# RWKV in three interleaved pieces, roots by logarithm and exponential, norms on ScalarE: a change to a two-layer Perceiver kernel

## The chip, the cores and the metric

The kernel runs on one core of a Trainium2 chip. The core has five engines with queues of their own: TensorE (PE in the profile, with its weight loads as PEld), VectorE (DVE), ScalarE (ACT), GpSimd (POOL) and SyncE (SP), which here only issues transfers. Each engine takes its instructions in the order in which the program lists them. The metric is the device time of one execution in microseconds (us).

## The reference, cut to what matters

The input is x of shape 64 x 32 x 256 and a context of 64 x 257 x 256. Six residual steps follow one another, each on a layer norm of x:

```python
x = x + L0_xattn(_layernorm(x), ctx, ctx, mask)      # stage 0: attention on the context
x = x + L0_attn(_layernorm(x), ...)                  # stage 1: RWKV
x = x + L0_ffn(_layernorm(x), Wg, We, be)            # stage 2: 8 experts, the best 2
x = x + L1_xattn(_layernorm(x), ctx, ...)            # stage 3: quantized attention
x = x + L1_attn(_layernorm(x), ...)                  # stage 4: state-space scan
x = x + L1_ffn(_layernorm(x), ...)                   # stage 5: 8 experts, all of them
return x
```

Stage 1, which the change cuts in three, has a time mix and a channel mix:

```python
h = layernorm(x, ln1_g, ln1_b); hh = time_shift(h)
xk, xv, xr = (h * m + hh * (1 - m) for m in (tm_k, tm_v, tm_r))
k, v, sr = xk @ Wk.T, xv @ Wv.T, sigmoid(xr @ Wr.T)
x = x + (sr * wkv(time_decay, time_first, k, v)) @ Wo.T       # a recurrence over 32 steps
h = layernorm(x, ln2_g, ln2_b); hh = time_shift(h)
xk, xr = (h * m + hh * (1 - m) for m in (cm_k, cm_r))
x = x + sigmoid(xr @ Wcr.T) * (square(relu(xk @ Wck.T)) @ Wcv.T)
```

## The kernel before

The 2048 rows (64 x 32) are cut into four blocks of 512 rows, each held in SBUF as four tiles of 128 rows x 256. x stays in SBUF from the first stage to the last. Every stage is a function that handles one block; `layers` (L1188) lists which stage of which block is written when, and a scheduler of the framework then puts each engine's instructions in an order of its own, with this list as priority. So stages of different blocks run mixed: stage 0 of one block beside stage 1 of the one before, and later stage 3 of one block beside the scan of stage 4 of another and the experts of stage 5 of a third.

Stage 0 (`_stage0`, L136) loads the context for four rows of the batch at a time (16 groups), and for each group computes the quantization scales of the context (L209), stores them to DRAM by a transfer on ACT's queue (L224), loads them back spread over the partitions, multiplies on POOL (L230), and attends (L236), with ACT doing exponentials and emptying PE's banks.

Stage 1 (`_stage1`, L340) is one function `block` per block (L470). It norms x, transposes it to channels (`norm_to`, L418), mixes with the shifted rows (L391), projects to k, v and r, runs the recurrence for two halves of the channels (`recur`, L432, mostly DVE, with a scratch pool of nine tiles), then projects back (`wo`, L490), norms again, and does the channel mix: `cr` (L503), then eight times `ck` (L511), Relu on ACT (L513), a square on POOL (L514) and `cv` (L523), all of the same block, in one go.

A norm is one DVE instruction (`_norm`, L114, and L429), x minus the mean times a reciprocal root; one set of four in stage 1 stands on POOL (L485). The mean and the variance come from L101 and L102. The reciprocal root (`_rsqrt`, L76) is a shift and a subtraction on the bits of the number, done on DVE (L84 to L87), and three Newton steps of four small instructions each on POOL (L89 to L92). A root for two sets of constants at once goes through it as one tile of eight columns.

Stage 4 has `ahead` (L968: norm, projection, convolution, softplus with an ACT logarithm at L1017 and an exponential at L1019), `gates` (L1026: four times Silu, straight from PE's bank, L1030) and `recur` (L1032): for 16 states POOL makes the input g (L1048), ACT the decay (L1052), DVE scans (L1053) and multiplies (L1054), and POOL sums (L1055); at the end it norms x and adds the output projection (L1062 to L1073). Stage 5 (L1081) has Gelu on ACT (L1164) between two rows of matmuls (L1160, L1168). ACT's functions come in tables; an instruction that loads one stands ahead of a function that the present table lacks.

Of the kernel before, what the change touches and what calls it, by code (L numbers as in the profile page):

```python
# [15 lines left out]
P = 128  # L16
# [39 lines left out]
def _consts(k):  # L56
    nc, c = k.nc, k.const
    k.ident = c.tile([P, P], F32, name="ident", tag="ident")
    make_identity(nc, k.ident)
    k.identb = c.tile([P, P], BF16, name="identb", tag="identb")  # L60
    nc.vector.tensor_copy(k.identb, k.ident)
    k.ones = c.tile([P, P], F32, name="ones", tag="ones")
    nc.gpsimd.memset(k.ones, 1.0)

    k.bmask = c.tile([P, 4], F32, name="bmask", tag="bmask")
    nc.vector.tensor_reduce(k.bmask, k.ident.rearrange("p (j n) -> p j n", n=32), AX.X, ALU.add)
    k.chan = c.tile([P, NCHAN], F32, name="chan", tag="chan")
    nc.scalar.dma_start(k.chan, k.i["chan"])
# [6 lines left out]

def _rsqrt(k, out, parts, tag, pool=None):  # L76


    nc, pool, f = k.nc, pool or k.small, out.shape[-1]
    n = out.shape[0]  # L80
    v, r, t = (pool.tile([P, f], F32, name=f"rs_{q}", tag=f"rs_{q}{tag}")[:n] for q in "vrt")
    at = 0
    for in_, scale, eps in parts:
        nc.vector.tensor_scalar(v[:, at : at + in_.shape[-1]], in_, scale, eps, ALU.mult, ALU.add)  # L84
        at += in_.shape[-1]
    nc.vector.tensor_scalar(r.bitcast(I32), v.bitcast(I32), 1, None, ALU.logical_shift_right)
    nc.vector.tensor_scalar(r.bitcast(I32), r.bitcast(I32), -1.0, 1597463007.0, ALU.mult, ALU.add)  # L87
    for step in range(3):
        nc.gpsimd.tensor_tensor(t, r, r, ALU.mult)  # L89
        nc.gpsimd.tensor_tensor(t, t, v, ALU.mult)  # L90
        nc.gpsimd.tensor_scalar(t, t, -0.5, 1.5, ALU.mult, ALU.add)
        nc.gpsimd.tensor_tensor(out if step == 2 else r, r, t, ALU.mult)  # L92

# [12 lines left out]
def _stats(k, tiles, tag, pool=None):  # L106

    mv = _moments(k, tiles, tag, pool)
    rstd = (pool or k.small).tile([P, 4], F32, name="rstd", tag=f"rstd{tag}")
    _rsqrt(k, rstd, [(mv[:, :, 1], 1.0, LN_EPS)], tag, pool)  # L110
    return mv, rstd


def _norm(k, out, x, mv, rstd, j):  # L114
    k.nc.vector.tensor_scalar(out, x, mv[:, j, 0:1], rstd[:, j : j + 1], ALU.subtract, ALU.mult)

# [19 lines left out]
def _stage0(k, pool):  # L136
# [163 lines left out]
    def steps():  # L300

        def of(dq, a, s, tag):
            _rsqrt(k, dq, [(s, 1.0 / D, RMS_EPS)], tag, blk)
            nc.vector.tensor_tensor(dq, dq, a, ALU.mult)
            nc.vector.tensor_scalar(dq, dq, 1e-5, 1.0 / 127.0, ALU.max, ALU.mult)
# [34 lines left out]
def _stage1(k, pool):  # L340
# [4 lines left out]
    nc, i = k.nc, k.i  # L345
    w, u, wk, sm1 = pool("w1", 1), pool("u1", 9), pool("wk1", 1), pool("small1", 2)
    pa, pb = pool("psa1", 2, space=bass.MemoryType.PSUM), pool("psb1", 2, space=bass.MemoryType.PSUM)
# [19 lines left out]
    for c in range(2):  # L367
# [4 lines left out]
        e2b.append(padded(f"e2b{c}", 0.0))  # L372
        e2bv.append(padded(f"e2bv{c}", 0.0))
    hT = padded("hT", 0.0, (2, 16, T + 1))

# [12 lines left out]
    def rows(name):  # L388
        return wk.tile([P, 4, D], F32, name=name, tag="rows", bufs=3)

    def shift_mix(names):  # L391


        def mix(name):
            return wk.tile([P, 2, 16, T], F32, name=name, tag="mix", bufs=3)

# [20 lines left out]

    def norm_to(xs, mean, scale, g, b):  # L418

# [8 lines left out]
        for j in range(4):  # L428
            nc.vector.tensor_scalar(hn[:, j, :], xs[:, j, :], mean[:, j, :], scale[:, j : j + 1], ALU.subtract, ALU.mult)  # L429
        _to_channels(k, [hn[:, j, :] for j in range(4)], evac, lambda shape, name: ps(name))  # L430
# [38 lines left out]

    def block(b):  # L470
        x = k.x[b]
# [4 lines left out]
        r8 = sm1.tile([P, 8], F32, name="r8", tag="r8")  # L476
        _rsqrt(k, r8, [(mv[:, :, 1], 1.0, LN_EPS), (mv[:, :, 1], 1.0 + LN_EPS, LN_EPS * LN_EPS)], "1", sm1)
        norm_to(x, mv[:, :, 0:1], r8[:, 4:8], "L0_attn_ln1_g", "L0_attn_ln1_b")
        xk, xv, xr = shift_mix(["L0_attn_tm_k", "L0_attn_tm_v", "L0_attn_tm_r"])
        rw = wk.tile([P, 2, BT], F32, name="rw", tag="rw", bufs=1)  # L480
        for c in range(2):
            recur(c, xk, xv, xr, rw)
        xn = rows("xn")
        for j in range(4):
            nc.gpsimd.tensor_scalar(xn[:, j, :], xs[j], mv[:, j, 0:1], r8[:, j : j + 1], ALU.subtract, ALU.mult)  # L485
        for j in range(0, 4, 2):
# [7 lines left out]

        mv2, rstd2 = _stats(k, [xn[:, j, :] for j in range(4)], "1b", sm1)
        norm_to(xn, mv2[:, :, 0:1], rstd2, "L0_attn_ln2_g", "L0_attn_ln2_b")
        xk, xr = shift_mix(["L0_attn_cm_k", "L0_attn_cm_r"])
        sg = rows("sg")
        for j in range(0, 4, 2):
            p = pa.tile([P, 2, D], F32, name="cr", tag="a")  # L500
            for f in range(2):
                for c in range(2):
                    nc.tensor.matmul(p[:, f, :], xr[:, c, (j + f) * P : (j + f + 1) * P], wT["cr"][:, c, :], start=c == 0, stop=c == 1)  # L503
            nc.scalar.activation(sg[:, j : j + 2, :], p, AF.Sigmoid)

        cvs = [pb.tile([P, 2, D], F32, name="cv", tag="b") for _ in range(2)]
# [23 lines left out]

    return block

# [120 lines left out]
def _stage3(k, w, tmp):  # L653
# [33 lines left out]
    def block(b):  # L687
# [11 lines left out]
        dq = k.small.tile([P, 4], F32, name="dq", tag="dq")  # L699
        _rsqrt(k, dq, [(mv[:, :, 1], 1.0 + RMS_EPS, RMS_EPS * LN_EPS)], "3")  # L700
        nc.vector.tensor_tensor(dq, dq, am, ALU.mult)
# [33 lines left out]
        dy = k.small.tile([P, 4], F32, name="dy", tag="dy")  # L735
        _rsqrt(k, dy, [(ss, 1.0 / D, RMS_EPS)], "3y")
        nc.vector.tensor_tensor(dy, dy, am, ALU.mult)
# [180 lines left out]
def _stage4(k, w, wk):  # L918
# [107 lines left out]
    def gates(v):  # L1026

        v.zs = wk.tile([P, C, BT], F32, name="zs", tag="zs", bufs=1)
        for c in range(C):
            nc.scalar.activation(v.zs[:, c, :], project(v, C + c, pp), AF.Silu, bias=_chan(k, "L1_attn_in_proj_b", C + c))  # L1030

# [49 lines left out]
def _stage5(k, w, out):  # L1081
# [21 lines left out]
    def block(b):  # L1103
# [28 lines left out]
        nc.vector.tensor_reduce(ms, sq, AX.X, ALU.add)  # L1132
        _rsqrt(k, ms, [(ms, 1.0 / E, F32_EPS)], "5r")
        nc.vector.tensor_tensor(lg, lg, over(ms), ALU.mult)
# [53 lines left out]
def layers(k, out):  # L1188
# [12 lines left out]
    with left0:  # L1201
        s1 = _stage1(k, opened(left0, "left"))
        with ExitStack() as es:
            s0, steps = _stage0(k, opened(es, "right"))
            s0(0)
            for b in range(1, NBLK):
                s0(b)
                if b < NBLK - 1:
                    s1(b - 1)
            steps()  # L1210
# [5 lines left out]
        s2 = _stage2(k, opened(right2, "right"))  # L1216
        s2(0)
        s3(0)
        s1(NBLK - 2)
        s1(NBLK - 1)  # L1220
    with right, left:
# [4 lines left out]
        with right2:  # L1226
            s2(1)
            v = {0: ahead(0)}
# [100 lines left out]
```

## Time and profile before

| what | value |
|---|---|
| time, median of 3 runs | 2092.72 us (2090.38 to 2098.58) |
| time of the profiled execution | 2096.84 us |
| span of its instructions | 2095.1 us |
| PE / DVE / ACT / POOL busy | 1644.2 / 1391.0 / 952.6 / 1013.9 us |
| granted TensorE clock, mean | 0.836 |
| loads of ACT tables | 112, of 1.283 us each |

The groups of the profile read: line, engine, operation, tile written <- tiles read, shapes, count | time busy in all, mean ns of one | idle time of the engine just before them, and what ended most of it. The waits read: engine and line that waited <- engine and line it waited for: us in all, how often, the longest. The windows read: from:to of the stretch, its length, then for each engine its busy time with its number of instructions, then the granted clock, the share of the transfer engines and GB/s.

By the time line, stage 0 ends at 394 us, block 0 leaves stage 3 at 714 us, the four scans of stage 4 run from 773, 1100, 1434 and 1748 us on, and the last 150 us are stage 5 of the last block.

### The profile page before, as it was taken

To read this page: it belongs to the slowest core of one execution; us is meant where nothing else is said; L and a number is where in the kernel's file an instruction comes from. 1 tells how busy PE (TensorE), PEld (TensorE's weight loads), DVE (VectorE), ACT (ScalarE), POOL (GpSimd) and SP (SyncE) were. 2 spreads that over 40 slices of the span, in tenths; PEclk is the share of its full clock that TensorE was granted. 3 is DMA by queue.
4 is the path that set the end of the run, shared out by engine and by line. 5 is a ranking of instruction groups with operands and counts; after the bars stand their busy time and mean duration, and the time that the engine had idled before them with its cause. 6 is when DMAs were issued, how large, how long until landed. Compare 5 with 4: busy or idle time off the path is not lost. (4 is left out here: it accounts for less than half of the span.)

```text
span 2095.1 us, 20245 instructions
## 1 busy us (share of the span) xinstructions
PE 1644.2 (78%) x6455; PEld 834.1 (40%) x6455; DVE 1391.0 (66%) x2444; ACT 952.6 (45%) x2009; POOL 1013.9 (48%) x1037
## 2 busy tenths in 40 slices
PE   4778966669979788656487798887888987787798
PEld 2334534335545434433234344433444433233343
DVE  5587584775584559889767988655888755876100
ACT  3445342304434174444146566356557445664232
POOL 4445445312121325667625777513767634998000
PEclk8677977889989898558687899888799887999799
DMA  7654232210001011121011232112232112332021
GB/s 239 219 182 144 91 120 80 79 34 21 21 21 43 17 42 51 30 61 61 0 50 53 80 91 90 31 41 65 71 88 73 49 31 66 89 111 77 30 81 40
DMA packets 87540, 149.93 MB, mean 72 GB/s; under 512 B 7672, under 2 KB 51978, under 8 KB 85386
## 3 DMA queue, kind: packets, MB, share of 16 engines
q1 hardware_dynamic: 84868, 147.69, 23.0%
q10 hardware_dynamic: 2566, 0.96, 0.2%
q8 instruction: 51, 0.84, 0.2%
q14 instruction: 55, 0.45, 0.1%
HBM read 137.71 MB, written 10.91 MB: 71 GB/s over the span
## 5 line engine op out<-in xcount | busy, mean ns | idle before, releaser
L1048 POOL TENSOR_TENSOR g<-dtx,bc 128x1024 f32<-128x1024 f32 x128 | 300.4, 2353 | 194.8 <-DVE h L1053 89.4
L1053 DVE TENSOR_TENSOR_SCAN h<-h,g 128x512 f32<-128x512 f32 x256 | 307.3, 1218 | 49.9 <-ACT h L1052 35.1
L1160 PE MATMUL up<-xT,w 128*128 128x512 f32 x512 | 288.1, 678 | 42.5 <-ACT hid L1162 37.3
L1055 POOL TENSOR_TENSOR xc<-xc,hc 128x1024 f32<-128x1024 f32 x128 | 301.0, 2356 | 26.5 <-DVE hc L1054 14.8
L1168 PE MATMUL acc<-hid,w 128*128 128x512 f32 x512 | 250.9, 610 | 15.8 <-ACT hid L1164 15.7
L1052 ACT ACTIVATE h<-dt,A 128x512 f32<-128x512 f32 x256 | 174.0, 692 | 184.5 <-DVE hc L1054 183.3
L1054 DVE TENSOR_TENSOR hc<-h,bc 128x512 f32<-128x512 f32 x256 | 169.7, 679 | 2.9 <-POOL xc L1055 0.5
L1160 PEld LDWEIGHTS up<-xT,w 128*128 128x128 f32 x512 | 97.3, 209 | 165.3 <-issue 79.2
L839 ACT ACTIVATE p<-sc,nm 128x256 f32<-128x256 f32 x256 | 117.6, 471 | 94.5 <-DVE nm L835 83.2
L1162 ACT ACTIVATE hid<-up,chan 128x512 f32<-128x512 f32 x128 | 87.2, 681 | 159.5 <-PE up L1160 159.4
L614 PE MATMUL weps<-we,xT 128*128 128x512 f32 x256 | 139.3, 665 | 17.2 <-DVE x L616 13.9
L1168 PEld LDWEIGHTS acc<-hid,w 128*128 128x128 f32 x512 | 94.1, 194 | 128.2 <-issue 96.3
L828 PE MATMUL sc<-kT,qm 32*128 32x256 f32 x512 | 131.6, 448 | 14.9 <-DVE od L867 11.5
L852 PE MATMUL pt_ps<-ident,p 128*128 128x128 f32 x512 | 97.0, 328 | 53.7 <-ACT p L839 26.6
L833 DVE TENSOR_REDUCE nm<-sc 128x2 f32<-128x512 f32 x128 | 86.3, 686 | 56.2 <-PE sc L828 55.1
L89 POOL TENSOR_TENSOR rs_t<-rs_r 128x4 f32<-128x4 f32 (+3 forms) x138 | 29.7, 218 | 183.1 <-DVE rs_r L87 157.0
L852 PEld LDWEIGHTS pt_ps<-ident,p 128*128 128x128 f32 x512 | 69.5, 165 | 107.1 <-ACT p L839 64.4
L828 PEld LDWEIGHTS sc<-kT,qm 32*128 32x128 f32 x512 | 81.5, 208 | 70.5 <-DVE od L867 20.7
L230 POOL TENSOR_TENSOR cT<-cT,scb 128x2056 f32<-128x2056 f32 x16 | 74.5, 4657 | 53.5 <-DMA scb<-scales 51.8
L1181 DVE SCALAR_TENSOR_TENSOR o<-rT,gt,x 128x256 f32<-128x256 f32 x16 | 7.7, 483 | 139.4 <-PE rT L1180 132.5
L854 ACT COPY pt<-pt_ps 128x512 f32<-128x512 f32 x128 | 74.0, 588 | 40.5 <-PE pt_ps L852 40.3
L514 POOL TENSOR_TENSOR kk<-kk 128x512 f32<-128x512 f32 x32 | 33.1, 1040 | 103.8 <-ACT kk L513 103.8
(389 smaller groups left out, 3218.7 us busy)
## 6 DMA issues: line engine op xcount, KB each, us to landing
bc<-rows SPq DMA_DIRECT2D x64, 512.0 KB
w<-in_L_ffn_w_dram SPq DMA_DIRECT2D x64, 512.0 KB
cT<-in_ctxT_dram SPq DMA_DIRECT2D x16, 1028.0 KB
cq<-cq SPq DMA_DIRECT2D x32, 514.0 KB
cn<-in_ctx_dram SPq DMA_DIRECT2D x64, 256.0 KB
scb<-scales SPq DMA_DIRECT2D x16, 514.0 KB
kb<-steps SPq DMA_DIRECT2D x16, 514.0 KB
x<-in_x_dram SPq DMA_DIRECT2D x4, 512.0 KB
```

What stands on the lines that cost most here:

```text
L614: nc.tensor.matmul(ps, xT[:, c, r], we[:, c, e : e + 2, :], start=c == 0, stop=c == 1)
L828: nc.tensor.matmul(sc[h][:, f, :], qm[r, e + f].rearrange("p l n g -> p (l n g)"), kTs[e][r, f, :], start=True, stop=True,)
L839: nc.scalar.activation(w_[:, f, h - h0, :], sc[h][:, f, :], AF.Exp, bias=nm[:, e + f, h : h + 1], accum_out=sm[:, e + f, h : h + 1],)
L852: nc.tensor.transpose(pt_ps[:, h, m, :], ws[e0, hp][:, f, h, m * P : (m + 1) * P], k.ident)
L1048: nc.gpsimd.tensor_tensor(g, dtx[:, c2 : c2 + 2], bc[:, 0:1, :].to_broadcast([P, 2, BT]), ALU.mult)
L1052: nc.scalar.activation(h, dt, AF.Exp, scale=A[:, c2 + c, n : n + 1])
L1053: nc.vector.tensor_tensor_scan(h, h, g[:, c, :], 0.0, ALU.mult, ALU.add)
L1054: nc.vector.tensor_tensor(hc[:, c, :], h, bc[:, 1, :], ALU.mult)
L1055: nc.gpsimd.tensor_tensor(y[:, c2 : c2 + 2], y[:, c2 : c2 + 2], hc, ALU.add)
L1160: nc.tensor.matmul(u, w1[e][:, c, q * P : (q + 1) * P], xT[:, c, :], start=c == 0, stop=c == 1)
L1162: nc.scalar.activation(hid[e][:, q, :], u, AF.Identity, bias=b1)
L1168: nc.tensor.matmul(acc[o], w2[e][:, q, o * P : (o + 1) * P], hid[e][:, q, :], start=n == H, stop=n == E * H + H - 1)
```

## The change

Stage 1 returns three functions in place of one: `time_mix`, `between` (output projection, second norm and receptance) and `channel_mix`. `layers` writes a block's channel mix behind the next block's time mix, and the time mix of the last block right behind the first block of stage 2. To hold two blocks at once, there are two hT tiles; the row tiles and the mixes share six buffers, both halves of the channels share one e2bv, and the scratch pool has eight tiles.

In all stages the reciprocal root is two ACT instructions, Ln(scale x + eps) and Exp(-0.5 x), with eps held in small tiles. A norm is one ACT instruction, scale times x plus offset, with the offset (minus mean times root) from one more small DVE instruction, `_offset`. `gates` empties the four banks with Identity and then takes Silu once over all four slices.

```diff
-def _rsqrt(k, out, parts, tag, pool=None):
...
-    nc.vector.tensor_scalar(r.bitcast(I32), v.bitcast(I32), 1, None, ALU.logical_shift_right)
-    nc.vector.tensor_scalar(r.bitcast(I32), r.bitcast(I32), -1.0, 1597463007.0, ALU.mult, ALU.add)
-    for step in range(3):
-        nc.gpsimd.tensor_tensor(t, r, r, ALU.mult)
-        nc.gpsimd.tensor_tensor(t, t, v, ALU.mult)
-        nc.gpsimd.tensor_scalar(t, t, -0.5, 1.5, ALU.mult, ALU.add)
-        nc.gpsimd.tensor_tensor(out if step == 2 else r, r, t, ALU.mult)
+def _rsqrt(k, out, in_, scale, eps):
+
+    k.nc.scalar.activation(out, in_, AF.Ln, bias=k.eps[eps][: in_.shape[0]], scale=scale)
+    k.nc.scalar.activation(out, out, AF.Exp, scale=-0.5)
...
+    _rsqrt(k, rstd, mv[:, :, 1], 1.0, LN_EPS)
+    _offset(k, mv[:, :, 0], mv[:, :, 0], rstd)
     return mv, rstd
+def _offset(k, out, mean, rstd):
+    k.nc.vector.scalar_tensor_tensor(out, mean, -1.0, rstd, ALU.mult, ALU.mult)
...
 def _norm(k, out, x, mv, rstd, j):
-    k.nc.vector.tensor_scalar(out, x, mv[:, j, 0:1], rstd[:, j : j + 1], ALU.subtract, ALU.mult)
+    k.nc.scalar.activation(out, x, AF.Identity, bias=mv[:, j, 0:1], scale=rstd[:, j : j + 1])
...
-    w, u, wk, sm1 = pool("w1", 1), pool("u1", 9), pool("wk1", 1), pool("small1", 2)
+    w, u, wk, sm1 = pool("w1", 1), pool("u1", 8), pool("wk1", 1), pool("small1", 2)
...
-        e2bv.append(padded(f"e2bv{c}", 0.0))
-    hT = padded("hT", 0.0, (2, 16, T + 1))
+        e2bv.append(e2bv[0] if c else padded("e2bv", 0.0))
+
+    hTs = [padded(f"hT{n}", 0.0, (2, 16, T + 1)) for n in range(2)]
...
-            nc.vector.tensor_scalar(hn[:, j, :], xs[:, j, :], mean[:, j, :], scale[:, j : j + 1], ALU.subtract, ALU.mult)
+            nc.scalar.activation(hn[:, j, :], xs[:, j, :], AF.Identity, bias=offset[:, j : j + 1], scale=scale[:, j : j + 1])
...
-            nc.gpsimd.tensor_scalar(xn[:, j, :], xs[j], mv[:, j, 0:1], r8[:, j : j + 1], ALU.subtract, ALU.mult)
+            nc.scalar.activation(xn[:, j, :], xs[j], AF.Identity, bias=o8[:, j : j + 1], scale=r8[:, j : j + 1])
...
-            nc.scalar.activation(v.zs[:, c, :], project(v, C + c, pp), AF.Silu, bias=_chan(k, "L1_attn_in_proj_b", C + c))
+            nc.scalar.activation(v.zs[:, c, :], project(v, C + c, pp), AF.Identity, bias=_chan(k, "L1_attn_in_proj_b", C + c))
+        nc.scalar.activation(v.zs, v.zs, AF.Silu)
...
-            s0(0)
-            for b in range(1, NBLK):
+
+            for b in range(NBLK - 1):
                 s0(b)
-                if b < NBLK - 1:
-                    s1(b - 1)
+                t = time_mix(b)
+                if b:
+                    channel_mix(b - 1, *c)
+                c = between(b, *t)
+            s0(NBLK - 1)
             steps()
...
         s2(0)
+        t = time_mix(NBLK - 1)
+        channel_mix(NBLK - 2, *c)
         s3(0)
-        s1(NBLK - 2)
-        s1(NBLK - 1)
+        c = between(NBLK - 1, *t)
+        s2(1)
+        channel_mix(NBLK - 1, *c)
...
         with right2:
-            s2(1)
             v = {0: ahead(0)}
```

## The prediction

> **What bounds the kernel now.** I read the engine totals first, then the same totals cut into six stretches at events I took from the time line (end of stage 0 at 394; block 0 leaves stage 3 at 714, block 1 at 1041, block 2 at 1378, block 3 at 1697), then the waits of the first stretch, then single groups.
>
> ```profile
> PE 1644.2 (78%) x6455; PEld 834.1 (40%) x6455; DVE 1391.0 (66%) x2444; ACT 952.6 (45%) x2009; POOL 1013.9 (48%) x1037
> ```
>
> No engine is full over the whole span; ACT, which is to receive work, is the emptiest.
>
> ```profile
> core 0: us, PE busy (x) PEld busy (x) DVE busy (x) ACT busy (x) POOL busy (x), PEclk, DMA share, GB/s
> 0.00:394.00 394.00, 289.46 (x1249) 153.01 (x1250) 254.97 (x427) 159.82 (x472) 184.64 (x245) 0.78 0.45 146
> 394.00:714.00 320.00, 257.95 (x1249) 148.34 (x1248) 206.00 (x468) 109.95 (x282) 77.16 (x142) 0.89 0.11 35
> 714.00:1041.00 327.00, 226.95 (x991) 122.77 (x990) 268.27 (x475) 136.51 (x316) 184.76 (x150) 0.70 0.14 39
> 1041.00:1378.00 337.00, 278.03 (x1122) 136.77 (x1121) 261.95 (x459) 183.20 (x362) 198.52 (x190) 0.85 0.22 65
> 1378.00:1697.00 319.00, 268.39 (x1097) 132.88 (x1095) 232.57 (x376) 181.21 (x360) 189.38 (x162) 0.86 0.21 60
> 1697.00:2095.00 398.00, 323.42 (x756) 140.33 (x754) 167.25 (x246) 181.95 (x218) 179.39 (x149) 0.92 0.24 69
> ```
>
> In the first stretch PE is idle 105 us and DVE 139: each waits for the other. In the third, DVE is the fullest engine (82%) and PE the idlest (69%). From 1041 on PE is 81 to 84% busy: there DVE relief is worth only what lies on the chain between two state-space scans.
>
> ```profile
> DVE sg L528 <- PE cv L523: 43.1, 3, 22.9
> POOL rs_t L89 <- DVE rs_r L87: 24.6, 10, 5.7
> ```
>
> Both are waits inside 0 to 395 us. The first is DVE standing still while PE does a channel mix, 43.1 us in three waits. The second is the root's iteration at the head of POOL's queue, waiting for DVE; it harms nobody, because POOL is empty.
>
> ```profile
> L839 ACT ACTIVATE p<-sc,nm 128x256 f32<-128x256 f32 x256 | 117.6, 471 | 94.5 <-DVE nm L835 83.2 <-DVE rs_v L84 8.0 <-DVE gt L1141 3.1
> L986 ACT ACTIVATE xc<-xpad,chan 128x512 f32<-128x512 f32 x16 | 13.0, 814 | 0.4
> L190 ACT ACTIVATE qT<-qps,chan 128x512 f32<-128x512 f32 x8 | 5.5, 687 | 4.5 <-PE qps L189 4.4
> L115 DVE TENSOR_SCALAR xn<-x,mv,rstd 128x256 f32<-128x256 f32 x64 | 31.1, 521 | 22.7 <-POOL rstd L92 17.6 <-DMA out_dram<-o 2.3 <-PE t_ps L1113 2.2
> L115 DVE TENSOR_SCALAR xe<-x,mv,rstd 128x256 f32<-128x256 f32 x16 | 25.8, 1645 | 2.0 <-POOL xc L1055 2.0
> L115 DVE TENSOR_SCALAR xe<-xe,mv,rstd 128x256 f32<-128x256 f32 x16 | 12.4, 823 | 7.0 <-POOL rstd L92 7.0
> ```
>
> The price of one norm on the two engines: on DVE 0.41 us where POOL is quiet (the time line), but 1.6 us on average at the end of a scan, where POOL runs 2.4 us instructions.
>
> ```profile
> 1423.00 1.28 ACT L1017 ACT_TABLE_LOAD   x1
> 1424.30 0.63 ACT L1017 ACTIVATE l__8548<-u__8547 128x512 f32<-128x512 f32 x1
> 1424.94 1.28 ACT L1019 ACT_TABLE_LOAD   x1
> 1426.24 0.63 ACT L1019 ACTIVATE u__8547<-l__8548 128x512 f32<-128x512 f32 x1
> ```
>
> A logarithm followed by an exponential, already there in the softplus: each has a table load ahead of it, 1.28 us, with 0.02 us around it.
>
> **RWKV in three pieces.** A channel mix is 32 matmuls of 0.601 us and 64 of 0.394 us: 44 us of PE. Now it follows its own block's time mix, so DVE has nothing; afterwards it stands behind the next block's time mix, whose recurrence is DVE work. Blocks 0 and 1 fall in the first stretch: of the 43.1 us that DVE waited I take 60%, 26 us, since in the compiled order 46 of the 48 products still stand in one run on PE and hold the attention of stage 0 as before. Block 2's falls beside block 3's time mix. Slices of 50 us show PE busy 22.4 at 400 to 450, where block 2's time mix and stage 2's gating have DVE busy 41.7; of the 27.6 us idle I take 12. Moved ahead by this are block 2's output projection, second norm and receptance (18 us of PE: 16 x 0.51, 8 x 0.34, 16 x 0.43), so by the order and these durations PE has 352 instead of 335 us ahead of stage 0's end. That is work moved, not added. Bounds: 0 to 70 us (43.1 + 27.6); taken: -38.
> The moves issue no DMA. SP's queue changes its order of stage 0's loads and stores by a place or two, with the same transfers. But ACT's queue issues the store of the scales that POOL's multiply waits for (51.8 us in nine waits in this stretch), and every ACT instruction that waits now holds it back; I leave that in the price of ACT's waits.
> The smaller buffers cost a little: e2bv is shared by the two channel halves, and with 8 instead of 9 scratch tiles the second half's first scan waits for the first half's last sum. One or two DVE instructions of 0.7 to 1.3 us, four blocks, two of them hidden by the other stages: +4.
>
> **Norms on ScalarE.** 144 norms. A 128x256 ACTIVATE with one pointer takes 471 ns, and the second pointer adds 814 - 687 = 127 ns: 0.58 to 0.60, so 85 us more on ACT. DVE loses 31.1 + 25.8 + 12.4 + 5.5 (L115) + 11.2 + 9.9 (L429) = 96 us and POOL 23.5 (L485). The third stretch is DVE's: there go 16 norms at a scan's end and in the next stages and some 20 small root instructions, up to 1.9 us each beside POOL, together near 25 us; I take -14. At the three later gaps between scans, four norms of 1.6 us are replaced by four of 0.6 on the path: -4 each, -12. In the first two stretches DVE's relief only makes room; 0 by itself, the cover being that DVE there waits 139 of 394 us; without that cover 40 us of ACT would stand on the path.
> Here a rule speaks against the change. The Trainium skill, ScalarE: Activation LUTs, section Rules for kernel authors, sends additions and multiplications to VectorE. The row agrees where POOL is quiet (0.41 against 0.6: 32 norms at scan ends would lose 6 us), and disagrees beside POOL (1.6 and 0.8 against 0.6). By the rule this part would be +27 us at the worst (144 x 0.19); by the rows it is -26. The rows decide.
>
> **Roots by Ln and Exp.** 46 roots cost 12 small instructions each on POOL (about 0.2 us each, 108 us in all) and three on DVE (39 us). From the last statistic at 1349.66 to the norm at 1353.79 it is 4.1 us. After: Ln 0.23 + load 1.28 + Exp 0.23 with the first load hidden where ACT is idle, 1.7 us; 3.0 us where it isn't, plus 0.2 for the new offset on DVE. So -2 to -1 us on a free ACT. About 30 roots stand on some stage's path, but PE fills a part of these gaps: -20.
> Against that, ACT is in-order and feeds all others. The compiled order has 182 table loads instead of 112: 44 before Ln and 41 before Exp, less 10 saved at the gates and 5 elsewhere. 70 x 1.283 = 90 us. With norms 85, roots 21 and gates 8, ACT rises from 45 to about 55%. The trace cannot show how long an Ln at ACT's head will wait for its statistics; POOL's own such wait is 157 us over the run (32 waits). Bounds: 0, if the scheduler places them late, and 100 us, if half of that and a quarter of the loads stall what follows (exponentials, evictions). Nearest to the 24.6 us of POOL's wait in the first stretch, I take +20.
> A second rule: the same page, section Table sets, says one named set holds exp and ln, so a pair needs one load. By it 41 loads would go, -53 us of ACT, and a root would be 1.3 us shorter. The two loads at 1423.00 and 1424.94 and the compiled order say it does not happen here. And its section on ACT_TABLE_LOAD prices a switch at 2.66 us with a drain; 70 switches would be 186 us. The trace shows 1.28 and no drain. By these two prices my +20 would be 0 or near +60.
>
> **Gates.** Silu once over four slices: 14 loads become 4 (-12.8 us of ACT) and four ACTIVATEs of 1.91 us come in (+7.6). -3 at most of it on a scan's start: -2.
>
> **The sum.** -38 + 4 - 26 - 20 + 20 - 2 = -62 us; the list order is set without these traces and will lose some of the overlap it plans, so I keep four fifths: -50. The profiled execution took 2096.8 us for a span of 2095.1, 4.1 above the median of 2092.7. 2096.8 - 50 - 4 = 2043.
>
> **The rivals.** *ACT becomes the hold-up* (slower). Place: 0 to 714 us, where by the orders ACT's work goes from 315 to 431 us and 44 of the 70 loads fall. ACT empties all of PE's banks there, and an Ln waiting for statistics stops the attention's exponentials and copies and the scale stores. Some 82 us of gain stand against ACT's 212 us of new work (order durations); it decides from about 45% of that on the path. At 60%: 2093 - 82 + 127 = 2138. For it: PE and DVE wait for ACT and each other already. Against: ACT is 59% idle there.
> *The gain is given back at the next meeting point* (no change). By order, 692 instead of 667 us of PE work stand before block 0 leaves stage 3, so the state-space scans start no sooner; only the later 12 + 14 us of PE work shrink, and PE sets the pace. Then some -10 from the norms, + 8 for ACT: 2091.
> *The DVE relief counts in full* (faster still): -96 - 39 of DVE, half on the path, plus -62 from the pieces: 1970.
>
> **Chances.** Forecast 0.52, full relief 0.08, given back 0.13, ACT 0.27. Below 1990 I leave about 0.07, above 2130 0.12. A difference of about 0.5% (10 us) is what a measurement of this kernel can tell from none: faster 0.60, the same 0.13, slower 0.27.
>
> **What would show it.** Right: DVE's wait for the channel mix in the first 395 us falls under 20 us; stage 0 ends before 390 with the second norm of block 2 behind it; ACT near 1140 busy with 182 loads; POOL under 900; block 0 leaves stage 3 by 680. Wrong: long waits of ACT for mv at L82, of PE for ACT's copies, or stage 0 ending after 410; then ACT is the hold-up. If block 0 leaves stage 3 at 710 although stage 0 ended early, it was given back.

## The result, and the profile after

The changed kernel takes 2111.68 us (median; 2109.9 to 2114.33), the kernel before in the same session 2092.26 us. The ratio is 1.0081 with a 95% interval of 1.0055 to 1.0107: slower by 0.8%, some 17 us, where 2043 us and a gain of 50 had been forecast. Every ratio below is to the kernel before, run on the same chip in the same session, with its 95% interval in brackets. Where two ratios of different sessions are subtracted, the difference is given in us at 2095 us for 1, and is good to about 10 us.

The totals of the changed kernel (profiled execution 2110.53 us, span 2108.7, clock 0.837):

```profile
PE 1668.8 (79%) x6455; PEld 841.7 (40%) x6455; DVE 1287.5 (61%) x2194; ACT 1147.2 (54%) x2343; POOL 891.9 (42%) x474
```

Work moved much as forecast: DVE lost 104 us (forecast 96 + 39), POOL 122 and ACT gained 195. The relief was real, and the time did not fall. The windows are cut at the same events as before; the columns are those of the windows shown in the prediction:

```profile
0.00:423.00 423.00, 311.54 (x1305) 163.61 (x1305) 269.82 (x406) 237.73 (x604) 156.71 (x95) 0.82 0.41 135
423.00:754.00 331.00, 282.43 (x1273) 159.21 (x1272) 187.46 (x441) 139.78 (x331) 46.22 (x42) 0.85 0.11 35
754.00:1063.00 309.00, 222.50 (x939) 119.02 (x940) 237.04 (x406) 150.90 (x341) 168.83 (x78) 0.69 0.16 43
1063.00:1383.00 320.00, 265.39 (x1123) 130.18 (x1121) 229.76 (x393) 220.86 (x424) 180.14 (x94) 0.90 0.25 70
1383.00:1695.00 312.00, 256.22 (x1085) 126.67 (x1083) 215.45 (x345) 199.66 (x396) 174.21 (x86) 0.88 0.21 61
1695.00:2109.00 414.00, 330.75 (x737) 143.07 (x735) 147.95 (x208) 198.30 (x251) 165.82 (x80) 0.87 0.22 64
```

The first stretch has grown from 394 to 423 us, and PE has 1305 matmuls and 311.54 us of work in it, 22 us more than before (1249 and 289.46). The second is 11 us longer. The three middle stretches are 18, 17 and 7 us shorter, and the last is 16 us longer. So 40 us are lost before block 0 leaves stage 3, 42 come back, and the tail loses 16 again. PE's work follows the same course: 594 us of it now stand before block 0 leaves stage 3 (311.54 + 282.43), where 547 stood before, and the three middle stretches hold 29 us less.

The waits from the start to the end of stage 0 (who waited <- for whom: us, times, longest):

```profile
POOL pl L253 <- ACT s L248: 130.1, 16, 37.0
...
PE tps L120 <- ACT xn L112: 18.3, 1, 18.3
...
DVE sg L540 <- PE cv L535: 6.4, 4, 3.7
```

and two rows of the kernel before, to the end of its stage 0, beside which they are to be read:

```profile
POOL pl L256 <- ACT s L251: 49.7, 12, 9.6
...
PE tps L123 <- DVE xn L115: 22.7, 1, 22.7
```

DVE's wait for the channel mix, 43.1 us before, is 6.4: the overlap works. POOL's wait for ACT's exponential of stage 0 has grown from 49.7 to 130.1 us. That looks like an ACT that is late, but POOL also has less to do now, and a longer wait of an engine with time to spare need not cost anything. With the roots alone (`e2_roots`, first 430 us), a kernel that is faster than before, this wait has grown too:

```profile
POOL pl L247 <- ACT s L242: 77.9, 12, 32.6
```

PE's one long wait for a norm, 22.7 us when DVE made it, is 18.3 us now that ACT makes it. So these rows don't show what holds the front up; the experiments have to.

### The profile page after: what moved, and what is told of

The parts are those of the page before. It is cut to its first block, busy times and chain, and to the rows that moved or that the text cites. A ratio compares the mean times of both kernels' runs of the same rounds, so it can differ in the third digit from the quotient of the medians.

```text
span 2108.7 us, 19805 instructions
## 1 busy us (share of the span) xinstructions
PE 1668.8 (79%) x6455; PEld 841.7 (40%) x6455; DVE 1287.5 (61%) x2194; ACT 1147.2 (54%) x2343; POOL 891.9 (42%) x474
## 5 line engine op out<-in xcount | busy, mean ns | idle before, releaser
L1181 PE MATMUL acc<-hid,w 128*128 128x512 f32 x512 | 256.4, 619 | 30.0 <-ACT hid L1177 29.9
L626 PE MATMUL weps<-we,xT 128*128 128x512 f32 x256 | 151.6, 714 | 17.2 <-DVE x L628 16.6
L840 PE MATMUL sc<-kT,qm 32*128 32x256 f32 x512 | 139.6, 465 | 16.6 <-DVE od L879 8.7
L864 PE MATMUL pt_ps<-ident,p 128*128 128x128 f32 x512 | 92.6, 316 | 40.4 <-ACT p L851 26.6
L840 PEld LDWEIGHTS sc<-kT,qm 32*128 32x128 f32 x512 | 86.2, 215 | 70.2 <-DVE od L879 15.9
L1049 POOL TENSOR_TENSOR dtx<-xc,dt 128x2048 f32<-128x2048 f32 x4 | 18.0, 4507 | 213.6 <-DVE dt L1034 213.6
L628 DVE SCALAR_TENSOR_TENSOR x<-weps,pr,x 128x256 f32<-128x256 f32 x128 | 61.1, 477 | 34.3 <-PE weps L626 32.6
```

What stands on the lines that cost most here:

```text
L626: nc.tensor.matmul(ps, xT[:, c, r], we[:, c, e : e + 2, :], start=c == 0, stop=c == 1)
L840: nc.tensor.matmul(sc[h][:, f, :], qm[r, e + f].rearrange("p l n g -> p (l n g)"), kTs[e][r, f, :], start=True, stop=True,)
L864: nc.tensor.transpose(pt_ps[:, h, m, :], ws[e0, hp][:, f, h, m * P : (m + 1) * P], k.ident)
L1181: nc.tensor.matmul(acc[o], w2[e][:, q, o * P : (o + 1) * P], hid[e][:, q, :], start=n == H, stop=n == E * H + H - 1)
```

## The experiments

Events read from the time line of one profiled execution each, in us from the span's start. "Step" is the time from the start of one block's scan to that of the next; "tail" is from the end of the last scan to the first expert matmul of the last block. The row of `f3_neutral` tells how well such events repeat, since its instructions stand in the order of the kernel before: the two rows differ by 1 to 3 us up to stage 3, by up to 8 us in a single step, and by 3 us in the sum of the three steps. Differences of single steps below 8 us are therefore not read.

| kernel | time, us | ratio | stage 0 ends | block 0 leaves stage 3 | steps | tail |
|---|---|---|---|---|---|---|
| before | 2092.26 | 1 | 394 | 714 | 328, 333, 315 | 45 |
| changed | 2111.68 | 1.0081 | 423 | 754 | 318, 312, 310 | 60 |
| e1_split | 2109.42 | 1.0072 | 431 | 742 | 311, 326, 318 | 51 |
| e2_roots | 2086.56 | 0.9953 | 386 | 697 | 312, 335, 324 | 54 |
| e3_norms | 2113.54 | 1.0085 | 408 | 731 | 324, 327, 310 | 54 |
| e4_gates | 2112.79 | 1.0074 | 395 | 717 | 331, 336, 318 | 48 |
| f1_s0first | 2080.15 | 0.9908 | 357 | 707 | 320, 336, 314 | 46 |
| f2_rwkv_first | 2156.37 | 1.0273 | 483 | 798 | 326, 320, 315 | 44 |
| f3_neutral | 2095.36 | 1.0001 | 391 | 713 | 328, 325, 320 | 44 |
| f4_noload | 2034.85 | 0.9696 | 401 | 714 | 307, 304, 306 | 61 |
| g1_after_s0first | 2080.27 | 0.9914 | 373 | 696 | 302, 324, 323 | 57 |
| g2_s0first_roots | 2054.78 | 0.9802 | 353 | 677 | 312, 327, 310 | 59 |
| g3_noroots | 2123.96 | 1.0123 | 428 | 745 | 331, 328, 330 | 44 |
| g4_nogates | 2099.21 | 1.0011 | 422 | 754 | 313, 307, 310 | 56 |
| h1_nonorms | 2077.84 | 0.9924 | 410 | 732 | 313, 321, 316 | 42 |
| h2_gate4 | 2117.65 | 1.0106 | 395 | 717 | 330, 343, 319 | 53 |
| h3_best | 2073.39 | 0.9896 | 349 | 676 | 313, 337, 321 | 60 |
| i1_xe_dve | 2105.09 | 1.0051 | 421 | 752 | 319, 313, 309 | 52 |

### The four parts, each alone

Each starts from the kernel before and takes one part of the diff shown above: the three pieces with their buffers and list; the roots; the norms with `_offset`; the batched gate.

*Pieces:*

> Only the three RWKV pieces and their buffers; roots by Newton, norms and gates as before. If ACT's new work is what made the whole change slow, the pieces alone gain: 2055 to 2075 us, with stage 0 over by 390. If the pieces themselves are the loss (block 0 left stage 3 at 754 us instead of 714 in the changed kernel), this run shows it: 2105 to 2130, with block 0 leaving stage 3 near 745.

1.0072 [1.0046, 1.0098]. DVE's wait for the channel mix falls to 8.9 us, and RWKV of block 3 is projected out at 536 us instead of 612; but stage 0 ends at 431 instead of 394. The steps are 21 us shorter in all, so most of the 28 us lost up to the end of stage 3 come back later. The piece that was to bring most of the gain is a loss by itself.

*Roots:*

> Only the roots by Ln and Exp; one RWKV piece, norms on DVE, gates as before. If the table loads and ACT's waits are the loss: 2120 to 2150, some 190 table loads, and the serial stretch from the last output projection of stage 4 to the last block's first expert matmul grows by 8 us or more. If the pieces are the loss: 2085 to 2100.

0.9953 [0.9937, 0.997]: faster, though the table loads rise from 112 to 199. Stage 0 ends 8 us earlier, block 0 leaves stage 3 17 us earlier. In the tail 9 us are lost.

*Norms:*

> Only the norms on ACT with the offset on DVE; Newton roots, one RWKV piece. By the sum on record -26 us: 2065 to 2075, nearly all between 714 and 1700 us. If a norm on ACT stands in the queue behind other ACT work and holds PE's transposes: 2095 to 2115.

1.0085 [1.0054, 1.0115]. The three steps between scans are together 15 us shorter, near the 12 forecast for them; the single steps lie within what repeats. Stage 0 ends 14 us later, block 0 leaves stage 3 17 us later, and the tail is 9 us longer. PE's waits for a norm before it can transpose, to the end of stage 0, first in the kernel before, then here:

```profile
PE tps L123 <- DVE xn L115: 22.7, 1, 22.7
PE tps L123 <- DVE hn L429: 10.0, 3, 5.5
```

```profile
PE tps L128 <- ACT xn L120: 22.9, 1, 22.9
PE tps L128 <- ACT hn L434: 9.3, 3, 5.3
```

They sum to 32.7 us on DVE and 32.2 on ACT: PE does not wait longer for the norms themselves, so the loss in front must come by another way.

*Gate:*

> Only Silu once over four slices. Both theories: within 5 us of before, 2088 to 2094, with about 20 table loads fewer.

1.0074 [1.0048, 1.01], against the forecast of a small gain. The loads did fall, to 90. Nothing in the front moves; the three steps are together 9 us longer and the tail 3.

### The list order of the pieces

`f1_s0first` has the same three pieces and buffers as `e1_split`; only the list differs: stage 0 of a block stands ahead of the time mix of the block before, and block 2's pieces behind the first attention of stage 3.

```diff
-            for b in range(NBLK - 1):
-                s0(b)
-                t = time_mix(b)
-                if b:
-                    channel_mix(b - 1, *c)
-                c = between(b, *t)
-            s0(NBLK - 1)
+            s0(0)
+            for b in range(1, NBLK):
+                s0(b)
+                if b == NBLK - 1:
+                    channel_mix(b - 2, *c)
+                    break
+                t = time_mix(b - 1)
+                if b > 1:
+                    channel_mix(b - 2, *c)
+                c = between(b - 1, *t)
             steps()
...
         s2(0)
-        t = time_mix(NBLK - 1)
-        channel_mix(NBLK - 2, *c)
         s3(0)
-        c = between(NBLK - 1, *t)
+        t = time_mix(NBLK - 2)
+        c = between(NBLK - 2, *t)
+        t = time_mix(NBLK - 1)
+        channel_mix(NBLK - 2, *c)
+        c = between(NBLK - 1, *t)
         s2(1)
```

> Only the RWKV in three pieces with its buffers, as in the first run of the pieces alone (2109 us), but the list is changed: stage 0 of block b+1 stands ahead of the time mix of block b, as it stood ahead of RWKV in the kernel before, and block 2's pieces come behind the first attention of stage 3. Theory: the pieces overlap well and the loss comes from the list order alone, since stage 3 of block 0 needs the end of all of stage 0. Then the DVE's wait for the channel mix stays under 15 us, stage 0 ends at 385 to 400 us (not 431), the first scores of stage 3 come before 505 us (not 536), block 0 leaves stage 3 before 722 us, and the time is 2085 to 2100 us. Rival: the pieces themselves, or the shared buffers, hold stage 0 up (PSUM, DVE, POOL taken by two blocks at once): stage 0 ends at 410 us or later whatever the order, and the time stays at 2105 to 2118 us.

0.9908 [0.9882, 0.9935], 2080 us, and stage 0 ends at 357, earlier than forecast. DVE's wait for the channel mix in the first 440 us is 14.0 us, so the overlap is kept. The first two stretches of `e1_split` and then those of `f1_s0first`, to the end of stage 0 and to where block 0 leaves stage 3:

```profile
0.00:431.00 431.00, 312.51 (x1305) 168.31 (x1305) 282.91 (x477) 177.69 (x495) 217.34 (x270) 0.79 0.42 134
431.00:742.00 311.00, 272.19 (x1272) 155.37 (x1272) 194.15 (x483) 95.53 (x264) 70.92 (x141) 0.89 0.11 35
```

```profile
0.00:357.00 357.00, 262.88 (x1173) 134.65 (x1174) 235.80 (x407) 154.42 (x464) 178.88 (x230) 0.81 0.50 162
357.00:707.00 350.00, 292.97 (x1356) 170.34 (x1354) 220.12 (x506) 117.80 (x294) 99.52 (x169) 0.89 0.10 30
```

In the one 1305 matmuls stand ahead of the end of stage 0, in the other 1173. Stage 3 of block 0 needs what `steps` makes, and `steps` needs stage 0 of all four blocks, so RWKV work of later blocks that is put ahead of that end delays stage 3. Not all of the delay gets through: stage 0 ends 74 us earlier in `f1_s0first`, block 0 leaves stage 3 35 us earlier, with 556 us of PE work before it in place of 585, and the three steps are then 15 us longer, because some of the work is still to be done there.

`f2_rwkv_first` is the converse: the uncut stage 1 of the kernel before, only listed earlier.

```diff
-            s0(0)
-            for b in range(1, NBLK):
+            for b in range(NBLK - 1):
                 s0(b)
-                if b < NBLK - 1:
-                    s1(b - 1)
+                s1(b)
+            s0(NBLK - 1)
             steps()
...
         s3(0)
-        s1(NBLK - 2)
         s1(NBLK - 1)
```

> The converse: the kernel before with RWKV in one piece, and only its place in the list changed: RWKV of block b stands behind stage 0 of block b and ahead of stage 0 of block b+1, block 2's too. Theory that the list order decides: stage 0 ends at 415 to 450 us (394 before), the first scores of stage 3 come at 520 to 560 us (496 before), and the time is 2102 to 2130 us, though nothing is cut in pieces. Rival that the pieces or buffers decide: stage 0 still ends at 400 us or earlier and the time is 2087 to 2100 us.

1.0273 [1.0224, 1.0323]: 57 us slower, stage 0 ends at 483 us. The size was underestimated, the direction is the theory's: the place in the list, not the cutting, costs.

`g1_after_s0first` gives the whole changed kernel the list of `f1_s0first`.

> The changed kernel whole, with the list order of the faster run of the pieces: stage 0 of the next block ahead of the time mix, block 2's pieces behind the first attention. Theory: the list order is the one step that turned the change into a loss; the order alone was worth 29 us on the pieces, so the time is 2075 to 2090 us, stage 0 ends at 375 to 395 us and block 0 leaves stage 3 by 725 us. Rival: ScalarE's longer queue (roots, norms, table loads beside stage 0's attention) holds stage 0 up whatever the list: it ends at 405 us or later, and the time is 2095 to 2112 us.

0.9914 [0.9881, 0.9947], with stage 0 ending at 373 us. Against the changed kernel that is 35 us for an edit of the list alone, and the sign of the whole change turns. The same edit on the pieces alone was worth 34.

### The roots and their table loads

`f4_noload` replaces the two functions of each root by two that load no table here; the roots are left out and become a constant.

```diff
-    k.nc.scalar.activation(out, in_, AF.Ln, bias=k.eps[eps][: in_.shape[0]], scale=scale)
-    k.nc.scalar.activation(out, out, AF.Exp, scale=-0.5)
+    k.nc.scalar.activation(out, in_, AF.Identity, bias=k.ones[: in_.shape[0], 0:1], scale=0.0)
+    k.nc.scalar.activation(out, out, AF.Copy, scale=0.25)
```

> The changed kernel, with logarithm and exponential of each root replaced by an Identity and a Copy on ScalarE that give a constant (the roots are left out of the computation); the same instructions in the same places, with 95 table loads in place of 182. 87 loads of 1.28 us are 112 us of ScalarE. Theory that the loads sit on the chain at the front and in the tail: the time falls by 15 to 30 us, to 2082 to 2097 us, and the tail from the end of the last scan to the first expert matmul falls from 60 us to 50 us or less. Rival that the loads lie in ScalarE's gaps and the loss comes from the order of the pieces: 2104 to 2114 us, with stage 0 still ending at 415 us or later.

0.9696 [0.9647, 0.9745]: 81 us below the changed kernel, far more than either theory allowed. In the changed kernel these are the loads ahead of Ln (L82) and Exp (L83); here both groups are absent:

```profile
L82 ACT ACT_TABLE_LOAD x44 | 56.5, 1283 | 5.0 <-DMA steps<-dT 3.9 <-ACT scT L219 0.3
...
L83 ACT ACT_TABLE_LOAD x41 | 52.6, 1283 | 0.7
```

87 loads fewer are 112 us of ACT, and the time fell by 81: 0.93 us for each load of 1.283, although ACT is busy only 54% of the span. That fits loads that stand in the chain from a statistic to its norm, where ACT's idle time elsewhere doesn't help. The kernel's values differ too, and so does its compiled order in places, so it isn't shown that all 81 us are loads. But up to the start of the second scan fewer than 50 instructions of each engine stand elsewhere, and there `f4_noload`, with 62 loads fewer so far, is already 53 us ahead (1068 us against 1121). One part of the expectation failed outright: the tail stayed at 61 us, so it isn't the loads that make it long.

`g3_noroots` is the changed kernel with Newton's steps, 97 loads.

> The changed kernel with the old Newton roots (97 table loads in place of 182), norms on ScalarE, the gate batched and the three pieces kept. Theory that the loads are what the roots cost here (leaving the loads out saved 76 us): 2085 to 2104 us, below the changed kernel. Rival that Newton's steps on GpSimd cost as much as the loads, as in the kernel with the roots alone, which was 10 us faster than before: 2112 to 2130 us.

1.0123 [1.0077, 1.0169]: 9 us above the changed kernel, but the two intervals overlap, so which of the two roots is dearer here isn't settled. Against two functions without loads, Newton's steps cost some 89 us in this kernel and Ln with Exp some 81.

`g2_s0first_roots` puts the roots on `f1_s0first`; norms and gate are as in the kernel before.

> The pieces with stage 0 first, and the roots by logarithm and exponential; the norms on VectorE and GpSimd and the gate chunk by chunk as in the kernel before. If the two gains add (0.9908 and 0.9953 of the kernel before) the ratio is 0.986, some 2067 us, with stage 0 ending at 345 to 357 us and block 0 leaving stage 3 by 695 us. Rival: with the pieces overlapped ScalarE has no gaps left at the front for 198 table loads, the gain of the roots is gone: 2078 to 2095 us.

0.9802 [0.9749, 0.9854], 2054.78 us, the fastest full version here. On top of the pieces in good order the roots are worth 22 us, where they were worth 10 alone; with some 12 us of uncertainty in the 22, it isn't shown that they are worth more here.

### The norms

`h1_nonorms` is the changed kernel with the norms back on DVE and POOL.

> The changed kernel with the norms on VectorE and GpSimd as in the kernel before; pieces, list order, roots and batched gate kept. If the single effects of those three add (+15, -10, +15), this takes 2112 to 2124 us: the norms then gain a few us inside the changed kernel, since the late stage 0 is decided by the list order and not by ScalarE. Rival: the norms cost in the changed kernel what they cost alone (17 us): 2090 to 2102 us, with stage 0 ending some 10 us earlier than the changed kernel's 423 us.

0.9924 [0.9881, 0.9966]. The norms on ACT cost the changed kernel some 33 us, more than the rival's 17. Stage 0 ends 13 us earlier and block 0 leaves stage 3 22 us earlier; the tail is 18 us shorter, and the three steps are 10 us longer. The norm itself took what was forecast for it on ACT; its commonest group in the changed kernel:

```profile
L112 ACT ACTIVATE xn<-x,mv,rstd 128x256 f32<-128x256 f32 x64 | 34.3, 590 | 29.4 <-PE beps L621 19.6 <-DMA out_dram<-o 8.5 <-DVE mv L108 1.2
```

So the sign and the size of the norms' part are shown, alone and in the whole. The way by which they cost it is not: a queue of ACT that serves the rest later would do it, and so would a new order that the scheduler makes of such an edit (see the gate below). No run separates the two.

`i1_xe_dve` puts back one norm, that at the scan's end:

```diff
-            _norm(k, xn[j], xs[j], v.mv, v.rstd, j)
+            nc.vector.tensor_scalar(xn[j], xs[j], v.rstd[:, j : j + 1], v.mv[:, j, 0:1], ALU.mult, ALU.add)
```

> The changed kernel with only the norm at the scan's end (x into xe) back on VectorE, as scale times x plus offset; all other norms stay on ScalarE. Theory that this norm on ScalarE lets TensorE reach the first half of the output projection early, then stand idle for 3.8 us and run what follows at half clock: the granted clock in the 15 us behind the last scan is 0.9 to 1.0 (0.50 in the changed kernel), the tail from the scan's end to the first expert matmul 42 to 52 us (60), and the time 2092 to 2104 us. Rival that tail and clock come from wherever the scheduler puts the expert matmuls: tail still 56 us or more, 2106 to 2116 us, and stage 0 ends at 423 us in either case.

1.0051 [1.0032, 1.0071]: lower by some 6 us, between the two forecasts, and the interval overlaps that of the changed kernel. The tail is down to 52. Behind the last scan PE has the same instructions in the same order in both. PE's time line behind the last scan, first in the changed kernel, then in `i1_xe_dve` (start, duration, engine, line, what, count, idle time ahead and who ended it):

```profile
1915.77 2.08 PE L1078 MATMUL outps<-w_L_attn_out_projT,xc 128*128 128x256 f32 x4 [3.79 <-POOL xc L1071]
1917.78 1.22 PE L1079 MATMUL outps<-brows,ones 1*128 1x256 f32 x2
1918.92 2.08 PE L1078 MATMUL outps<-w_L_attn_out_projT,xc 128*128 128x256 f32 x4
```

```profile
1912.81 1.13 PE L1078 MATMUL outps<-w_L_attn_out_projT,xc 128*128 128x256 f32 x4 [0.89 <-POOL xc L1071]
1913.88 0.69 PE L1079 MATMUL outps<-brows,ones 1*128 1x256 f32 x2
1914.50 1.13 PE L1078 MATMUL outps<-w_L_attn_out_projT,xc 128*128 128x256 f32 x4
```

The same four matmuls take 2.08 us behind an idle time of 3.79 and 1.13 behind one of 0.89. The 15 us behind the scan, again in this order:

```profile
1916.00:1931.00 15.00, 15.00 (x31) 9.02 (x32) 3.10 (x9) 0.00 (x0) 0.40 (x1) 0.50 0.00 1
```

```profile
1913.00:1928.00 15.00, 15.00 (x47) 8.09 (x47) 4.91 (x15) 6.27 (x11) 4.22 (x7) 1.00 0.00 1
```

A granted clock of 0.50 against 1.00. It goes with a tail that is 8 us longer, of the 18 us between the changed kernel and `h1_nonorms`; what brings it isn't the idle time alone (see the last section).

`h3_best` adds only that norm on ACT to `g2_s0first_roots`.

> The fastest version so far (pieces with stage 0 first, roots by logarithm and exponential; ratio 0.980), with one norm on ScalarE: that at the end of the scan, x into xe, which took VectorE 1.6 to 2.4 us a tile beside GpSimd. If the forecast 12 us at three gaps hold, or the 4 to 6 us a gap that the run with all norms on ScalarE showed: ratio 0.974 to 0.977, some 2042 to 2048 us. Rival: the first tile of xe is made under the scan's last steps anyway, or ScalarE has no room there: 2052 to 2060 us.

0.9896 [0.9852, 0.994]: slower than without it by some 20 us, where 7 to 13 were to be gained; the two intervals just touch. The clock behind its last scan is 0.50 too (1.00 without the norm), yet the tail is only 1 us longer. Most of the loss is in the steps of the middle scans, 337 and 321 for 327 and 310, and why isn't settled.

### The gate

`f3_neutral` projects the four chunks of the gate in the order 3, 2, 1, 0.

> The kernel before with one edit that adds and removes no work: the four chunks of the gate z in stage 4 are projected in the order 3, 2, 1, 0. What it measures is how far the compiled order, and with it the time, moves when nothing but the list is touched. Theory that the batched gate's 14 us are a matter of where the scheduler then puts everything: the time differs from the kernel before by 5 us or more in one or the other direction. Rival that the batched gate costs by itself: this kernel is within 4 us of the kernel before (2089 to 2101 us), with scans of 259, 232, 228 and 174 us within 5 us each.

1.0001 [0.9977, 1.0025]. The compiled order turned out the same but for the chunk's number: the 2444 instructions of DVE, the 1897 of ACT without its loads and the 1037 of POOL follow one another as in the kernel before. So this shows only that two equal orders take equal times; of what another order does it says nothing.

`g4_nogates` is the changed kernel with Silu chunk by chunk.

> The changed kernel with Silu of the gate chunk by chunk, as in the kernel before; 195 table loads in place of 182. If batching the gate costs some 14 us by itself, as it did in the kernel before, this takes 2094 to 2101 us, with the second and third scan some 10 us shorter each. If those 14 us came from where the scheduler put the instructions of stage 3 and of the scan that time, they do not come back: 2106 to 2125 us (13 table loads more are 17 us of ScalarE).

1.0011 [0.9982, 1.0039]: 15 us come back, as in the kernel before, though it has 13 loads more.

`h2_gate4` empties the banks with Identity and then takes four short Silus:

```diff
-            nc.scalar.activation(v.zs[:, c, :], project(v, C + c, pp), AF.Silu, bias=_chan(k, "L1_attn_in_proj_b", C + c))
+            nc.scalar.activation(v.zs[:, c, :], project(v, C + c, pp), AF.Identity, bias=_chan(k, "L1_attn_in_proj_b", C + c))
+        for c in range(C):
+            nc.scalar.activation(v.zs[:, c, :], v.zs[:, c, :], AF.Silu)
```

> The kernel before with the gate's chunks evacuated by Identity, and then four Silus of 512 columns, each free to be placed (111 table loads, 112 before): no batch, no load saved, 16 more ScalarE instructions of 0.69 us, and again a compiled order that differs from before in hundreds of places. Theory that the batch is what costs (one Silu of 1.9 us that needs all four projections and blocks ScalarE's queue): 2093 to 2102 us. Rival that it is the new compiled order of scan and stage 3, however it arises: 6 us or more away from the kernel before, on either side, with the steps from one scan's start to the next away from 328, 333 and 315 us by 3 us or more.

1.0106 [1.0054, 1.0158]: slower without any batch, so the loss does not need the one long Silu. What is left is the evacuation in two steps or the order of scan and stage 3 that the scheduler makes of it (some 500 of DVE's 2444 instructions stand elsewhere); which of the two stays open.

## Why the prediction was wrong, point by point

- **Pieces, -38 and buffers, +4.** The mechanism was right and the sign of its worth wrong. The wait for the channel mix went away (forecast under 20 us, measured 6.4). The step that failed is "PE has 352 instead of 335 us ahead of stage 0's end. That is work moved, not added": it was seen and given no price. Measured, 22 us more of PE work stand ahead of that end, the end comes 29 us later and block 0 leaves stage 3 40 us later, since stage 3 needs that end. The moved work did come back, as "moved, not added" says, but in the later steps, and with the pieces alone not in full (21 of 28 us). The term was +15 us alone; with stage 0 listed first, the same pieces and buffers gave -19, so the list and not the cutting made the sign.
- **Norms, -26.** The durations held: 590 ns on ACT, forecast 580 to 600, and the three steps are together 15 us shorter, where 12 were forecast. What failed is "0 by itself" for the first two stretches, with the cover that DVE waits there anyway. With the norms alone block 0 leaves stage 3 17 us later, and the whole part is +18 us alone and +33 in the changed kernel, near the 40 that the prediction named for the case without cover. DVE's idle time was no cover for work that goes to ACT; why ACT's own idle time was none stays open. The rule weighed there (the Trainium skill, ScalarE: Activation LUTs, Rules for kernel authors: additions and multiplications go to VectorE) had given +27 and was set aside by comparing durations of one instruction. The runs side with the rule in the sign; its reason, a faster instruction, is not what they show, for PE's waits for the norms were 32.2 us on ACT and 32.7 on DVE.
- **Roots, -20, and ACT's waits, +20.** The net of 0 was -10 alone, -9 in the changed kernel, where the intervals overlap, and -22 on the pieces in good order. The two terms were mis-sized by about as much, in opposite directions: leaving the loads out took 81 us off where +20 was taken for all of ACT's new waits, inside the bound of 100, and the kernel with Newton's steps takes 89 us more than the one with neither, where 20 was taken for their removal. That the net came out near was luck. The price of a load was right (1.283 us), and one load for both functions (Table sets, same page) is not what happens here: the roots have 44 and 41 loads.
- **Gate, -2.** Measured +15 twice. The forecast counted instructions and left out what the two-step evacuation and the new order of scan and stage 3 could cost; the runs don't say which of them it is.
- **The signs given.** ACT busy 1147 us (forecast near 1140) with 182 loads and POOL 892 (under 900) came true; stage 0 ended at 423, not before 390; block 0 left stage 3 at 754, not by 680. "Wrong: stage 0 ending after 410; then ACT is the hold-up" named the right sign and the wrong first cause: with ACT left as it was, the pieces alone end stage 0 at 431.
- **The rivals.** *ACT becomes the hold-up* fits the sizes of the norms (+33) and of the loads, though the waits don't prove it for the norms; it is not needed for the 29 us at stage 0's end. *Given back at the next meeting point* had the mechanism, 692 instead of 667 us of PE work before block 0 leaves stage 3 (measured 594 and 547), but took it for a gain that is lost; it was a loss. *DVE relief in full* was far off: 104 us less of DVE went with a longer time.
- **Sums.** Three are off and turn nothing. By the profile Newton's steps take 118 us on POOL and 45 on DVE, where 108 and 39 are given. The ACT rival breaks even at 82 of 212, which is 39% and not 45%. The full-relief rival adds -62 for the pieces, which is the sum of all parts.

Measured alone, the four parts add to +38 us (+15, -10, +18, +15); together they are +17, so they do not simply add. Against the terms of the sum the largest errors are the pieces (49 us) and the norms (44 alone, 59 in the changed kernel), then the gate (17); the roots erred by 10 the other way.

## What to carry to other kernels

Ask of each moved piece what point everything behind it waits for, and count the work that the new order puts ahead of that point: here an edit of the list alone was worth 34 us on the pieces and 35 on the whole. An engine at half load is not free: the norms on ACT cost 18 to 33 us although ACT was the emptiest engine, and leaving 87 table loads of 1.283 us out took off 81 of 112 us. Test the parts singly before the whole; the best version here keeps the pieces and the roots, drops norms and gate, and lists stage 0 first: 2054.78 us, ratio 0.9802.

## What the runs showed of the hardware that was not expected

The granted clock behind the last scan of the changed kernel was 0.50 for some 17 us, although PE was busy nearly throughout by the profile. The idle time of 3.79 us ahead of it doesn't explain this by itself: behind the last scan the clock fell in `i1_xe_dve` as well, after an idle time of 2.14 us, and in `h2_gate4`, whose norms stand on DVE, after one of 2.59 us. The stretches at half clock in the changed kernel, in `i1_xe_dve` and in `h2_gate4`:

```profile
1914.30:1931.00 16.70, 15.23 (x31) 9.25 (x32) 3.10 (x9) 0.00 (x0) 2.10 (x2) 0.50 0.00 1
```

```profile
1908.40:1911.60 3.20, 3.20 (x7) 1.69 (x5) 3.20 (x3) 0.00 (x0) 3.20 (x3) 0.50 0.00 0
```

```profile
1941.60:1955.00 13.40, 13.40 (x29) 7.97 (x27) 3.10 (x9) 0.00 (x0) 1.43 (x3) 0.50 0.01 1
```

In `i1_xe_dve` the clock was back at 1.00 before 1913 us, as its row further up shows. So what differs is how long the clock stays down. The Trainium skill (TensorE: Matmul & The Clock Gate, Part 1) puts the fall to half rate at about 3.4 us of idleness and the return at about 3.4 us of sustained work. Neither agrees with these rows: two falls came behind shorter idle times, and 13.40 us of a busy PE did not bring the clock back in `h2_gate4`. About a quarter of the matmuls behind the last scan work on a single row (1x256); whether that counts is not tested.
